# Cross-attention in a decoder layer: exponentials without maxima behind a check, keys by position a batch ahead, queries turned by VectorE and DRAM

## Chip, cores and metric

The kernel runs on one core of a Trainium2 chip. The metric is the device time of one execution in microseconds (us), lower is better. The engines are TensorE (PE; its weight loads are listed as PEld), VectorE (DVE), ScalarE (ACT), GpSimd (POOL) and the queue that issues most transfers, SyncE (SP).

## What is computed

One pre-norm decoder layer in fp32: x of 16 batches x 128 rows x 1024 columns, self-attention, cross-attention to a context of the same shape, and a feed-forward network (FFN) with int4 weights of inner width 2752. The change is in the cross-attention, which treats the 128 rows as channels (c) and the 1024 columns as positions (n):

```python
qh = jnp.einsum('bcn,oc->bon', q, Wq).reshape(b, HEADS, DIM_HEAD, -1)   # 8 heads of 64
kh = jnp.einsum('bcn,oc->bon', k, Wk).reshape(b, HEADS, DIM_HEAD, -1)
vh = jnp.einsum('bcn,oc->bon', v, Wv).reshape(b, HEADS, DIM_HEAD, -1)
qh = jax.nn.softmax(qh, axis=-2) * SCALE      # over the 64 features of a head
kh = jax.nn.softmax(kh, axis=-1)              # over the 1024 positions
context = jnp.einsum('bhdn,bhen->bhde', kh, vh)
out = jnp.einsum('bhde,bhdn->bhen', context, qh)
out = jnp.einsum('bcn,oc->bon', out.reshape(b, HIDDEN, -1), Wo) + bo[None, :, None]
norm = jnp.maximum(jnp.sqrt(jnp.sum(out * out, axis=1, keepdims=True)), 1e-12)
return out / norm * g * np.sqrt(DIM)
```

q is the layer-normalised x, k and v are the context. The result is added to x.

## The kernel before

The program has three stages on one core: self-attention in four groups of four batches (lines 289 to 510), cross-attention batch by batch (512 to 916), and the FFN, whose matrix products are done by a fast (Strassen-Winograd) scheme in blocks (918 to 1770). The stages overlap at their ends.

**Order of work.** `InOrder` (line 50) keeps TensorE's and VectorE's instructions in the order in which the program writes them. In cross-attention that order is made by a small clock: `later(n, fn)` puts a function on a list, `tick()` runs those that are due. A batch has four key units and four query units in turn, a tick after each: eight ticks. After the last batch each matrix product of the FFN's first block ticks once (`beside`), and when the list is empty `attention_done` closes the stage's pools and starts the preparation of the later FFN weights. SP issues its transfers in order; a transfer that waits holds up those behind it. Batches 8 to 15 come first, then 0 to 7.

**Key unit** (`key_unit`, line 669). It makes 128 of the 512 key features for all 1024 positions: two matmuls into a pair of PSUM banks (`kq`), the row maximum on VectorE (`knmax`), and the exponential with that bias and an accumulated sum on ScalarE (`ke`, line 678). The context product needs positions on the partitions, so two ticks later VectorE turns 32x32 blocks (`kt`), SP stores the tile in DRAM (`kd`, line 692) and loads it back with the blocks in place (`kh`, line 696).

**Query unit** (`query_unit`, line 701). It makes all 512 features for 256 positions, positions on the partitions: two matmuls, the maximum of each head (`qmx`), the subtraction on VectorE (`qe`), the exponential on ScalarE (line 715). Two ticks later `weigh` sums each head (`qden`), takes the reciprocal and lets GpSimd multiply (line 721). Four ticks later `turn` makes eight 128x128 transposes on TensorE (`tr`, with the identity), and two ScalarE copies (`qs`, line 731).

**The rest of a batch.** `context` multiplies the turned keys with the context (`mm<-kh,cxt`, 32 instructions of 256 columns for each batch; each fp32 matmul is recorded as two) and `mix` folds in the product of Wv and Wo (`g_sb`, made once) and the key sums' reciprocal, giving `m_sb`. `project_out` multiplies `m_sb` with the turned queries in four pieces, takes the column norms with a matmul against ones, and then scales, adds to x, takes the statistics for the FFN's normalisation and turns the rows for it (`turn_rows`, tile `xt`, through DRAM). Blocks of these rows are loaded for the FFN by `block_loads`.

Tile pools of the stage lie on two sides: those of the units (cx, weights, ke, kt, qe, and `kq` in four PSUM banks) are given back when the last unit is written, the others when `attention_done` runs.

Of the kernel before, what the change touches and what calls it, by code (L numbers as in the profile page):

```python
# [33 lines left out]
Q = 32  # L34

# [30 lines left out]
def decoder_layer(  # L66
# [22 lines left out]
    out: bass.AP,  # L89
):  # L90
    nc = tc.nc
# [474 lines left out]
    def turn_rows(b, xn, pool):  # L566

        kt = pool.tile([P, 4, 2 * JC, Q], F32, name="xt")
        vector.transpose(
            kt.rearrange("p c m t -> p m c t"), xn.rearrange("p m (c i) -> p m c i", c=4)  # L570
        )
        xt = xt_all[PASSES.index(b - b % HB)][b % HB]
        for a in range(4):
            nc.sync.dma_start(
                xt[a].rearrange("c i n j t -> i c (n j t)"),
                kt[ts(a, Q)].rearrange("i c m t -> i c (m t)"),
            )
# [21 lines left out]
    bkt = unit_pool("b_kt", 2)  # L599
    b3 = unit_pool("b_3", 3)  # L600
    bpk = unit_pool("b_k", 2, space=PSUM)
    bs = side_pool("b_s", 1)
    bct = side_pool("b_ct", 3)
    bkh = side_pool("b_kh", 3)
    bqs = side_pool("b_qs", 7)
    b1 = side_pool("b_1", 1)
    b2 = side_pool("b_2", 2)
    bps = side_pool("b_ps", 2, space=PSUM)
    btr = side_pool("b_tr", 2, space=PSUM)
# [16 lines left out]
    if True:  # L626
# [15 lines left out]
        vector.memset(ones, 1.0)  # L642

# [25 lines left out]
        def key_unit(c_sb, oc, kh, part, ksum):  # L669
            ps = bpk.tile([P, 2, 512], F32, name="kq")  # L670
            for h in range(2):
                tensor.matmul(
                    ps[:, h, :], wk_sb[:, ts(oc, P)], c_sb[:, ts(h, 512)], start=True, stop=True
                )
            nmax = small.tile([P, 1], F32, name="knmax")
            vector.tensor_reduce(nmax, ps, AX.XY, ALU.max, negate=True)
            ke = b0.tile([P, 2, 512], F32, name="ke")
            nc.scalar.activation(ke, ps, AF.Exp, bias=nmax, accum_out=ksum[:, oc : oc + 1])  # L678

            if oc % 2 == 0:
                part[:] = [dram.tile([4, Q, 4, 2, NB, Q], F32, name="kd", tag="kd", bufs=2)]
            (kd,) = part

            def turn():
                kt = bkt.tile([P, 4, NB, Q], F32, name="kt")
                vector.transpose(
                    kt.rearrange("p c n j -> p n c j"),
                    ke.rearrange("p h (n c j) -> p (h n) c j", c=4, j=Q),  # L690
                )
                nc.sync.dma_start(kd[:, :, :, oc % 2].rearrange("p i c n j -> (p i) c n j"), kt)
                if oc % 2 == 1:
                    t = kh[oc // 2] = bkh.tile([P, 4, 2, NB, Q], F32, name="kh")
                    for c in range(4):
                        nc.sync.dma_start(
                            t[ts(c, Q)], kd[:, :, c].rearrange("p i o n j -> i p o n j")
                        )

            later(2, turn)  # L700

        def query_unit(xn, pair, qs):
# [8 lines left out]
            mx = small.tile([P, 2 * HEADS], F32, name="qmx")  # L711
            vector.tensor_reduce(mx, heads, AX.X, ALU.max)
            qe = b3.tile(wide, F32, name="qe")
            vector.tensor_tensor(qe, heads, mx.unsqueeze(2).to_broadcast(wide), ALU.subtract)
            nc.scalar.activation(qe, qe, AF.Exp)

            def weigh():
                den = small.tile([P, 2 * HEADS], F32, name="qden")
                vector.tensor_reduce(den, qe, AX.X, ALU.add)
                vector.reciprocal(den, den)  # L720
                nc.gpsimd.tensor_tensor(qe, qe, den.unsqueeze(2).to_broadcast(wide), ALU.mult)  # L721

            def turn():
                qt = bqs.tile([P, 4, 2 * P], F32, name="qs", tag="qs")
                qs.append(qt)
                qf = qe.rearrange("p (i r e) d -> p i r (e d)", i=2, e=2)
                for i in range(2):
                    tr = btr.tile([P, 4, P], F32, name="tr")
                    for r in range(4):
                        tensor.transpose(tr[:, r, :], qf[:, i, r], ident)  # L730
                    nc.scalar.copy(qt[:, :, ts(i, P)], tr)

            later(2, weigh)
            later(4, turn)

        def context(ct, kh, ksum, m_sb, when):

            kc = b1.tile([P, HIDDEN], F32, name="kc")
            bank = {}

            def piece(pair, part):
                if part == 0:
                    bank[pair] = bps.tile([P, HIDDEN // 2], F32, name="mm")
                ps = bank[pair]
                for nb in range(4 * part, 4 * part + 4):
                    tensor.matmul(
                        ps,
                        ct[:, nb, :],
                        kh[pair][:, :, :, nb, :].rearrange("n p o j -> n (p o) j"),
                        start=(nb == 0),  # L750
                        stop=(nb == NB - 1),
                    )
                if part == 1:

                    nc.scalar.copy(
                        kc[:, ts(pair, HIDDEN // 2)].rearrange("s (o p j) -> s o p j", o=2, j=Q),
                        ps.rearrange("s (p o j) -> s o p j", o=2, j=Q),
                    )

            def mix():  # L760
                D = DIM_HEAD
                krec = small.tile([P, 4], F32, name="krec")
                vector.reciprocal(krec, ksum)
                mp = bps.tile([P, 4, S], F32, name="mm")
                for r in range(4):

                    for e in range(2):
                        tensor.matmul(
                            mp[ts(e, D), r, :],
                            kc[:, ds(r * P + e * D, D)],  # L770
                            g_sb[:, 2 * r + e, :],
                            start=True,
                            stop=True,
                        )
                vector.tensor_tensor(
                    m_sb, mp, krec.unsqueeze(2).to_broadcast([P, 4, S]), ALU.mult
                )

            for k in range(4):
                later(when[k], lambda k=k: piece(*divmod(k, 2)))  # L780
            later(when[4], mix)

        def turned(b):
# [8 lines left out]
            later(2, lambda: turn_rows(b, xn, b1))  # L792
# [6 lines left out]
        def project_out(b, qs, m_sb, when):  # L799
            out, bank = {}, {}  # L800

            def piece(h, part):
# [6 lines left out]
                for r in range(4):  # L809
                    tensor.matmul(  # L810
                        ps[:, ts(part, 2 * P)],
                        m_sb[:, r, :],
                        qs[2 * h + part][:, r, :],
# [70 lines left out]
        for n in range(2 * BPT):  # L884
# [3 lines left out]
            )  # L888
        for k, b in enumerate(batches):
            kh, part, qs = {}, [], []  # L890
            ksum = b2.tile([P, 4], F32, name="ksum")
            m_sb = b1.tile([P, 4, S], F32, name="m_sb")

            if k + 2 < B:
# [945 lines left out]
```

## Time and profile before

| | |
|---|---|
| median of three runs | 2272.14 us (2271.86 to 2274.11) |
| the profiled execution | 2272.22 us, its span 2270.4 us |
| TensorE clock granted | 1.00 throughout |
| self-attention | about the first 250 us |
| cross-attention | its first key matmul starts at 252.9 us, its last key matmul at 784.9, its last projection matmuls at about 842 |
| FFN | its first product starts at 794.4 us; from 847 to the end it has TensorE alone |
| vector work for one batch in cross-attention | knmax, qmx 1192 ns each, qe 1225, qden 1205, kt 1230, four times each |

The profile is one execution taken by the hardware profiler. Rows of groups give line, engine, operation, output and input tiles, shape and number of instructions, then busy time and the mean of one in ns. Line 62 is the `InOrder` helper, so most TensorE and VectorE instructions of the stage are told apart by their tiles. The end of a matmul is modelled[...], so that the pace of a sequence is read from the starts. A wait is given as who waited for whom, the sum in us, how often, and the longest.

### The profile page before, as it was taken

What the parts mean: (1) busy time and instruction counts of PE and PEld (TensorE: products, weight loads), DVE (VectorE), ACT (ScalarE), POOL (GpSimd) and SP (SyncE); (2) the same over time, 40 slices, a digit from 0 to 9 for tenths busy, and PEclk for the clock granted to TensorE, in tenths of its full rate; (3) what the DMA queues carried; (4) which work ended last, traced back from release to release, by engine and by line L of the source; (5) the groups of instructions that cost most, each with busy time, mean ns of one, the idle gap of its engine ahead of it and who ended that gap; (6) DMA issues with size and microseconds to landing.
All of it is one profiled execution on the core that took longest, in us unless ns stands there. A gap on an engine that the chain in (4) does not pass through costs nothing.

```text
span 2270.4 us, 25324 instructions
## 1 busy us (share of the span) xinstructions
PE 2243.3 (99%) x8968; PEld 1598.7 (70%) x8968; DVE 1616.5 (71%) x2161; ACT 546.2 (24%) x861; POOL 473.7 (21%) x381
## 2 busy tenths in 40 slices
PE   8999999999999999999999999999999999999999
PEld 7556566666666664444684468888888688888888
DVE  6987788889889938665796658777777546544463
ACT  2111255665665551111111111121121100000000
POOL 5452122222222200000340034444443000000000
PEclk9999999999999999999999999999999999999999
DMA  6445266566688558788739943554554974434631
GB/s 248 159 135 183 93 168 183 169 195 193 169 241 224 156 167 276 265 273 269 231 119 276 287 135 122 185 194 145 184 191 149 339 235 149 140 121 145 224 116 38
DMA packets 276974, 425.22 MB, mean 187 GB/s; under 512 B 26736, under 2 KB 128496, under 8 KB 276720
## 3 DMA queue, kind: packets, MB, share of 16 engines
q1 hardware_dynamic: 250768, 377.71, 53.2%
q0 software_dynamic: 8064, 27.27, 3.3%
q10 hardware_dynamic: 18016, 18.62, 2.6%
q8 instruction: 72, 1.18, 0.2%
q14 instruction: 54, 0.44, 0.1%
HBM read 265.62 MB, written 157.35 MB: 186 GB/s over the span
## 4 chain that ended last, share of the span: by engine, by line
PE 91%; DVE 6%; issue 2%; DMA 1%; ACT 1%; POOL 0%; SPq 0%; DVEq 0%; POOLq 0%; ACTq 0%
PE po L1725 21%; PE q L62 20%; PE p L62 18%; PE mm L62 11%; PE kq L62 8%; PE mm L391 4%; PE tr L62 2%; PE p L1102 2%; PE mm L406 2%; DVE pa L62 1%; PE mm L287 1%; PE tr L338 1%; DVE ti L62 0%; DVE bnst L62 0%; DVE kt L62 0%
## 5 line engine op out<-in xcount | busy, mean ns | idle before, releaser
L62 PE MATMUL p<-b,w 128*128 128x512 f32 x560 | 246.4, 592 | 0.0
L62 PE MATMUL q<-ti,li 128*128 128x256 f32 x1008 | 232.2, 379 | 3.5 <-DVE ti L62 2.8
L62 PEld LDWEIGHTS q<-ti,li 128*128 128x128 f32 x1008 | 191.0, 190 | 31.3 <-issue 2.8
L62 POOL TENSOR_TENSOR li<-w 128x512 f32<-128x512 f32 x84 | 118.2, 1409 | 430.8 <-DMA wu<-pc 235.6
L62 PEld LDWEIGHTS p<-b,w 128*128 128x128 f32 x560 | 106.4, 190 | 133.1 <-issue 128.7
L1725 PE MATMUL po<-wc,lc 128*128 128x256 f32 x840 | 183.4, 379 | 0.0
L721 POOL TENSOR_TENSOR qe<-qe,qden 128x1024 f32<-128x1024 f32 x64 | 121.7, 1901 | 270.0 <-DVE qden L62 160.7
L62 PE MATMUL p<-T,w 128*128 128x512 f32 x400 | 177.2, 592 | 0.0
L1725 PEld LDWEIGHTS po<-wc,lc 128*128 128x128 f32 x840 | 159.6, 190 | 21.8
L62 ACT COPY k<-q 128x512 f32<-128x512 f32 x126 | 73.8, 585 | 400.0 <-PE q L62 400.0
L62 PEld LDWEIGHTS p<-T,w 128*128 128x128 f32 x400 | 76.0, 190 | 95.7 <-issue 95.4
L1725 PE MATMUL po<-wq,lq 128*128 128x256 f32 x560 | 126.7, 379 | 0.3 <-issue 0.3
L62 PEld LDWEIGHTS mm<-qs,m_sb 128*128 128x128 f32 x512 | 97.2, 190 | 38.9 <-issue 28.2
L62 PE MATMUL kq<-cx,wk_sb 128*128 128x512 f32 x256 | 120.8, 594 | 3.7 <-ACT ke L678 3.7
L62 PE MATMUL mm<-kh,cxt 128*128 128x256 f32 x512 | 122.6, 382 | 1.0 <-PE mm L62 0.5
L62 PE MATMUL kq<-wq_sb,xn 128*128 128x512 f32 x256 | 120.4, 593 | 0.0
L62 PE MATMUL mm<-qs,m_sb 128*128 128x256 f32 x512 | 120.3, 379 | 0.0
L62 PEld LDWEIGHTS mm<-kh,cxt 128*128 128x128 f32 x512 | 95.9, 190 | 31.3 <-issue 18.6
L1725 PEld LDWEIGHTS po<-wq,lq 128*128 128x128 f32 x560 | 106.0, 190 | 15.9 <-issue 0.9
L62 DVE TENSOR_TENSOR pa<-pa,sz 128x1024 f32<-128x1024 int32 x86 | 112.6, 1309 | 2.5
L391 PE MATMUL mm<-xnT,wqkv_sb 128*128 128x512 f32 (+1 forms) x320 | 112.6, 508 | 0.0
L62 DVE TENSOR_REDUCE qmx<-kq 128x16 f32<-128x1024 f32 x64 | 76.3, 1192 | 47.6 <-PE kq L62 47.6
(191 smaller groups left out, 3858.7 us busy)
## 6 DMA issues: line engine op xcount, KB each, us to landing
w<-wu SPq DMA_DIRECT2D x140, 256.0 KB, 3.3
lq<-h SPq DMA_DIRECT2D x140, 256.0 KB, 4.5
w<-wg SPq DMA_DIRECT2D x138, 256.0 KB, 2.8
kd<-kt SPq DMA_DIRECT2D x64, 512.0 KB, 3.5
kh<-kd SPq DMA_DIRECT2D x128, 256.0 KB, 5.6
h<-hc SPq DMA_DIRECT2D x80, 256.0 KB, 2.9
wq<-wd SPq DMA_DIRECT2D x70, 256.0 KB, 5.0
h<-h SPq DMA_DIRECT2D x60, 256.0 KB, 3.4
```

The lines of the kernel that those rows point to most:

```text
L62: return lambda *args, **kw: self._tc.keep_in_program_order(fn(*args, **kw))
L287: tensor.matmul(ps, oT[:, d, ts(b % BPT, S)], wo_d[d][:, ts(h, 512)], start=(d == 0), stop=(d == 1),)
L338: nc.tensor.transpose(tr[:, j, :], xn[:, ts(4 * h + j, P)], ident)
L391: nc.tensor.matmul(ps[:, tokens], wqkv_sb[:, f, c, :], xnT[:, c, tokens], start=(c == 0), stop=(c == CC - 1),)
L406: nc.tensor.matmul(ps, xnT[:, c, ts(i, S)], wqkv_sb[:, 4:6, c, :], start=(c == 0), stop=(c == CC - 1),)
L721: nc.gpsimd.tensor_tensor(qe, qe, den.unsqueeze(2).to_broadcast(wide), ALU.mult)
L1102: tensor.matmul(ps, wt[:, j, :], T[q][:, :, j], start=(first == q and j == 0), stop=(q in (2, 3, 4) and j == JC - 1), skip_group_check=True,)
L1725: nc.tensor.matmul(bank[:, i, :], l[:, ts(i, S)], w,  start=(start and c == 0 and i % 2 == 0), stop=(stop and c == len(pairs) - 1), skip_g ...
```

## The change

Four things are changed in cross-attention.

- **No maxima.** With `plain` set, keys and queries are exponentiated as they come. The sums and their reciprocals are added up on GpSimd (`note`), and after the stage `raise_flag` counts the partitions in which both totals are at most 1e18. At the end of the program every engine reads that count; if it is below 128, the whole layer is run again with the maxima (`plain` unset), otherwise that second copy of the program is jumped over.
- **Keys by position.** A key unit now makes all 512 features for 256 positions, with positions on the partitions. The exponentials are used as they lie, as the moving operand of the context product with 512 columns (`use`); key sums over positions are added on VectorE and finished on TensorE by matmuls against a column of ones in `mix`. The keys' trip through DRAM goes.
- **A batch ahead.** Key units for the next batch stand between the query units of this one; four key units with four ticks stand before the first batch. In the last batch there are query units alone.
- **Queries through VectorE and DRAM.** `turn` now transposes 32x32 blocks on VectorE (`kt`), stores to DRAM (`kd`), and a tick later loads four pieces (`qs`). The transposes on TensorE and the ScalarE copies go. The projection reads `qs` in runs of 32 elements.

The times in ticks of the later steps, the pools and their numbers of buffers follow. The diff, cut to its core:

```diff
-    bkt = unit_pool("b_kt", 2)
+    bek = unit_pool("b_ek", 3)
+    bas = unit_pool("b_as", 1)
     b3 = unit_pool("b_3", 3)
+    bkt = side_pool("b_kt", 3)
...
-    bct = side_pool("b_ct", 3)
-    bkh = side_pool("b_kh", 3)
-    bqs = side_pool("b_qs", 7)
+    bct = side_pool("b_ct", 2)
+    bqs = side_pool("b_qs", 5)
...
-    bps = side_pool("b_ps", 2, space=PSUM)
-    btr = side_pool("b_tr", 2, space=PSUM)
+    bps = side_pool("b_ps", 3, space=PSUM)
...
+        def note(*both):
+            if plain:
+                for t, v in zip(totals, both):
+                    t = t[:, : v.shape[1]]
+                    nc.gpsimd.tensor_tensor(t, t, v, ALU.add)
+
+        def raise_flag():
+
+            within = [small.tile([P, 1], F32, name=f"within{n}") for n in range(2)]
+            for w, t in zip(within, totals):
+                vector.tensor_reduce(w, t, AX.X, ALU.add)
+                vector.tensor_scalar(w, w, LIMIT, None, ALU.is_le)
+            vector.tensor_tensor(within[0], within[0], within[1], ALU.mult)
+            ps = bps.tile([P, 1], F32, name="mm")
+            tensor.matmul(ps, ones, within[0], start=True, stop=True)
+            vector.tensor_copy(flag, ps[0:1])
...
+        def key_unit(ctx, p, st):
...
             ps = bpk.tile([P, 2, 512], F32, name="kq")
-            for h in range(2):
+            for i in range(2):
+                chunk = c_sb[:, ts(2 * p + i, P)]
+                if plain:
+                    tensor.matmul(ps[:, i, :], chunk, wk_sb, start=True, stop=True)
+                    continue
...
+            ek = bek.tile([P, 2, 512], F32, name="ek")
+            nc.scalar.activation(ek, ps, AF.Exp)
+
+            def use():
+                if p == 0:
+                    st["ps"] = bps.tile([P, HIDDEN], F32, name="kx", bufs=1)
+                    st["ek"] = ek
+                for i in range(2):
+                    tensor.matmul(
+                        st["ps"],
+                        ct[:, 2 * p + i, :],
+                        ek[:, i],
+                        start=(p == i == 0),
+                        stop=(p == 3 and i == 1),
+                    )
+                if p == 1:
+                    st["sum"] = bas.tile([P, 2, 512], F32, name="ksum")
+                    vector.tensor_tensor(st["sum"], st["ek"], ek, ALU.add)
+                elif p > 1:
+                    vector.tensor_tensor(st["sum"], st["sum"], ek, ALU.add)
+                if p == 3:
+                    t = st["sum"]
+                    vector.tensor_tensor(t[:, 0], t[:, 0], t[:, 1], ALU.add)
+                    st["kc"] = b1.tile([P, HIDDEN], F32, name="kc")
+                    nc.scalar.copy(st["kc"], st["ps"])
+                    later(2, lambda: mix(st))
+
+            later(2, use)
+
+        def mix(st):
+
+            D = DIM_HEAD
+            ks = bps.tile([P, 4], F32, name="mm")
+            for r in range(4):
                 tensor.matmul(
+                    ks[:, r : r + 1], st["sum"][:, 0, ts(r, P)], ones[:, 0:1], start=True, stop=True
                 )
+            ksum, krec = (small.tile([P, 4], F32, name=name) for name in ("ksum", "krec"))
+            vector.tensor_copy(ksum, ks)
+            vector.reciprocal(krec, ksum)
+            note(ksum, krec)
...
             qe = b3.tile(wide, F32, name="qe")
-            vector.tensor_tensor(qe, heads, mx.unsqueeze(2).to_broadcast(wide), ALU.subtract)
-            nc.scalar.activation(qe, qe, AF.Exp)
+            if plain:
+                nc.scalar.activation(qe, heads, AF.Exp)
...
             def turn():
-                qt = bqs.tile([P, 4, 2 * P], F32, name="qs", tag="qs")
-                qs.append(qt)
-                qf = qe.rearrange("p (i r e) d -> p i r (e d)", i=2, e=2)
-                for i in range(2):
-                    tr = btr.tile([P, 4, P], F32, name="tr")
-                    for r in range(4):
-                        tensor.transpose(tr[:, r, :], qf[:, i, r], ident)
-                    nc.scalar.copy(qt[:, :, ts(i, P)], tr)
+                kt = bkt.tile([P, 4, NB, Q], F32, name="kt")
+                vector.transpose(
+                    kt.rearrange("p c n j -> p n c j"),
+                    qe.rearrange("p h d -> p (h d)").rearrange("p (n c j) -> p n c j", c=4, j=Q),
+                )
+                kd = dram.tile([4, Q, 4, NB, Q], F32, name="kd", tag="kd", bufs=3)
+                nc.sync.dma_start(kd.rearrange("a i c n j -> (a i) c n j"), kt)
+
+                def load():
+                    qt = qs[pair] = bqs.tile([P, 4, NB, Q], F32, name="qs", tag="qs")
+                    for c in range(4):
+                        nc.sync.dma_start(
+                            qt[ts(c, Q)], kd[:, :, c].rearrange("a i n j -> i a n j")
+                        )
+
+                later(1, load)
 
             later(2, weigh)
-            later(4, turn)
+            later(wait, turn)
...
-                        m_sb[:, r, :],
-                        qs[2 * h + part][:, r, :],
+                        st["m"][:, r, :],
+                        qs[2 * h + part].rearrange("p a (i r) j -> p r i a j", r=4)[:, r],
...
+            if len(ahead) == 2:
+                when = (12, 13, 14, 15, 16, 1, 1)
+            elif ahead:
+                when = (12, 13, 14, 15, 16, 1, 0)
             else:
-                when = (8, 9, 11, 12, 13), (14, 14, 15, 15, 16, 1, 0)
+                when = (10, 10, 11, 11, 12, 1, 0)
...
             for oc in range(4):
+                if ahead:
+                    key_unit(ctxs[ahead[0]], oc, keys[ahead[0]])
+                    tick()
+                query_unit(xns[b], oc, qs, 4 if len(ahead) == 2 else 3)
                 tick()
...
-        decoder_layer(tc, *args, res)
+        with tc.tile_pool(name="flag", bufs=1) as fp:
+            flag = fp.tile([1, 1], I32, name="flag")
+            decoder_layer(tc, *args, res, flag)
+            rows_within = nc.values_load(flag, min_val=0, max_val=P)
+
+            with tc.If(rows_within < P):
+                decoder_layer(tc, *args, res)
```

## Prediction

> **What bounds the kernel now.** I read the page's busy shares first, then the busy time by stretches, then one cross-attention batch in order of time on TensorE, then the waits of TensorE and of the SP queue.
>
> ```profile
> PE 2243.3 (99%) x8968; PEld 1598.7 (70%) x8968; DVE 1616.5 (71%) x2161; ACT 546.2 (24%) x861; POOL 473.7 (21%) x381
> ...
> PE 91%; DVE 6%; issue 2%; DMA 1%; ACT 1%; POOL 0%; SPq 0%; DVEq 0%; POOLq 0%; ACTq 0%
> ```
>
> TensorE is busy for all but 27 us. A busy PE need not be at its peak, so the next two views check it where the change is made. Stretches (columns: stretch, length, then busy us of PE, PEld, DVE, ACT, POOL with instruction counts, clock, DMA share, GB/s):
>
> ```profile
> 290.00:310.00 20.00, 16.93 (x64) 9.48 (x62) 18.93 (x22) 10.79 (x18) 6.26 (x4) 1.00 0.54 152
> ...
> 435.66:469.65 33.99, 33.99 (x150) 23.09 (x149) 29.99 (x36) 20.48 (x33) 8.79 (x6) 1.00 0.64 186
> 469.65:503.64 33.99, 33.99 (x149) 23.08 (x149) 29.99 (x36) 20.49 (x33) 8.78 (x6) 1.00 0.65 187
> ```
>
> A batch takes 33.99 us, with no hole on PE and VectorE (DVE) at 30.0. Only the first batches have holes. Inside a batch (start, length, what):
>
> ```profile
> 503.48 1.89 PE L62 MATMUL mm<-qs,m_sb 128*128 128x256 f32 x8
> 505.20 1.89 PE L62 MATMUL mm<-kh,cxt 128*128 128x256 f32 x8
> 506.93 1.04 PE L62 MATMUL tr<-ident,qe 128*128 128x128 f32 x8
> 507.80 1.88 PE L62 MATMUL kq<-wq_sb,xn 128*128 128x512 f32 x4
> 509.52 1.89 PE L62 MATMUL mm<-kh,cxt 128*128 128x256 f32 x8
> 511.25 1.88 PE L62 MATMUL kq<-cx,wk_sb 128*128 128x512 f32 x4
> 512.96 1.88 PE L62 MATMUL mm<-sq,ones 128*128 128x512 f32 x4
> ```
>
> Start to start, every group takes its columns at one rate: 4 passes of 512 in 1.72 us, 8 passes of 256 in 1.73, 8 transposes of 128 in 0.87 (506.93 to 507.80). An fp32 matmul is two passes, a transpose one. So this stage costs what TensorE is given, and a change is worth the passes that it removes. What PE waits for, and what SP waits for (sum us, times, longest us):
>
> ```profile
> PE kq L62 <- ACT ke L678: 3.7, 4, 1.6
> PE q L62 <- DVE ti L62: 3.3, 4, 2.4
> PE p L1102 <- DMA w<-wg: 1.7, 1, 1.7
> ```
> ```profile
> SPq L692 <- DVE kt L62: 280.8, 51, 16.0
> ...
> SPq L696 <- DMA kd<-kt: 69.0, 32, 3.2
> ```
>
> PE loses 3.7 us to key exponentials, all but 0.2 in the first batch, and 1.7 to the FFN's first weights. SP waits a lot, but in the stage's batches PE waits for what it then moves (kh) only once, for 0.2 us.
>
> **What the Trainium skill says.** "TensorE: Matmul & The Clock Gate", LDWEIGHTS, prices a weight load by its columns over 1.2, which is 107 ns for 128; the trace agrees in that 16 passes of 128 columns with a load each (line 421) took 1.78 us, 111 ns each. "VectorE: DVE Perf Modes", The three transpose paths, says that VectorE turns 32x32 blocks only, so a full turn needs another mover: here the kt groups (1230 ns for 128x1024) plus a store and loads through DRAM. "DMA: Bandwidth & Descriptors", Two DMAs through the same engine are not ordered, has the issuing engine wait for the first DMA's completion: the 69.0 us above. "Runtime: NRT & Kernel Launch", Instruction fetch mechanics, says that a taken branch to far code stalls for a fetch; no branch is in this trace.
>
> **The change, part by part** (16 batches).
>
> 1. *Query turns leave TensorE.* 4 units x 8 transposes per batch, 0.87 us per unit: 0.872 x 64 = 55.8 us removed, nothing of it beside other PE work. -55.8. The 128 ACT copies of them (593 ns) go too; ACT is not on the path.
>
> 2. *Key sums on TensorE.* The maxima's accumulated sums go; mix has four matmuls of one column, eight passes per batch. Each needs a 128-column load; with one column to compute, the load sets the pace. The trace shows no such matmul. Page price 107 ns: 128 x 0.107 = 13.7 us, which I take. Low end: the issue floor of the same page (Back-to-back issue gap, about 25 ns), 3.2 us. High end: the duration that the trace shows of one load, 190 ns, 24.3 us. **+13.7 (3 to 24)**. These wait for DVE's last half add of the sum; behind them on PE stand that mix and the next unit. DVE has from tick 8 to tick 2, two units and more on PE, for some 6 us of queued work, so I cost the wait at nothing; uncovered it would be at most the 1.2 + 0.7 us of those adds per batch.
>
> 3. *Context product.* 32 passes of 256 per batch become 16 of 512; by the rows above 1.73 against 1.72 us for the same columns. 0. The projection reads qs in runs of 32 floats as the context product read kh before, at the same 1.73. 0.
>
> 4. *DVE, ACT, POOL.* DVE loses per batch four knmax (1192 ns), four qmx (1192) and four qe subtractions (1225), 14.4 us, and gains three adds (1.22) and a half one (0.69), 4.4; the four transposes move from keys to queries. 30.0 - 14.4 + 4.4 = 20.0 us of a new period of 33.99 - 3.49 + 0.86 = 31.4. POOL gets ten small adds per batch: between 0.10 us (a one-element memset) and 1.03 (pow on four columns), so 1 to 10 us on top of 8.8; under 31.4 even so. All this is hidden by PE. If a tick's POOL work slips, the turn behind it slips, which is the rival below.
>
> 5. *DRAM trip.* SP issues per batch 4 kd stores, 16 qs loads, 4 xt, 2 ctx = 26 instead of 18; at about 0.45 us an issue (four take 1.73 to 1.75 us in SP's timeline) 12 us of 31. The loads wait for their store, with the next stores and ctx loads queued behind, but they now come a tick after it rather than at once. From the last turn (tick 11) to its use (tick 15) PE has nine 1.72 us groups, 15.5 us. The trip needs a transpose 1.23, store landing 3.5 and load landing 5.6 (the median of the larger kh loads): 10.3. Spare 5 us: 0.
>
> 6. *Start.* With keys a batch ahead and no maxima, an exponential follows its matmul at once and its bank comes free earlier. The four waits above and their like in the first 80 us (PE busy 73.8 of 80) should mostly go; the prologue of four key units may bring its own. **-3.5 (-5 to 0)**. The FFN's first weight tile waits for space that the last keys' input held; these keys now end a batch earlier. **-1 (-1.7 to 0)**.
>
> 7. *The flag.* raise_flag puts five small DVE ops and a matmul in program order in the FFN's first block: PE stands, with all later products behind it, until DVE has done them. Ahead on DVE is the last xt transpose (1.23) and up to two 0.69 us combinations. 1.23 + about 1.2 (five ops near the 253 ns of a 16-element reciprocal) + a PE drain of 0.17 = 2.6, plus half of a combination. **+3 (1 to 5)**.
>
> 8. *Branch at the end.* Every engine reads the flag and jumps over a second copy of the program. Not in the trace; the last matmul group starts at 2265.47 and the last outputs are issued at 2266.9, so part of it lies beside the 3.5 us of the last outputs' transfer. I take **+4 (1 to 10)**: one round trip of about a DMA landing (3 us) plus synchronisation. A gain is excluded, since the old end stays.
>
> Sum: -55.8 + 13.7 - 3.5 - 1 + 3 + 4 = -39.6. The profiled execution took 2272.2 us (span 2270.4, 1.8 around it), the same as the median of 2272.1: **2232.6 us**.
>
> **Rivals.**
> - *The trip sets the end (slower side).* Place: pieces at ticks 12 to 15, where PE meets qs. It costs only beyond 15.5 us; then each batch waits once. With 20 us: 15 batches x 4.5 = 68, so 2232.6 + 68 = 2300. It decides against the change from 15.5 + 39.6/15 = 18.1 us. For: SP's queue is in order and longer, DMA share reaches 0.81 and 0.90 in the stretches around 622 to 690. Against: same bytes as before, DVE is relieved, 5 us spare.
> - *Part of the gain is lost in small waits* (DVE, POOL or qs, 1 us per batch): 2232.6 + 16 = 2249. For: DVE order holds scale, weigh, turn and mix together at ticks 1 and 2. Against: 11 us of DVE slack per batch.
> - *More than forecast:* one-column matmuls near the floor (-10.5), flag and branch at their low ends (-5): 2217.
> - *The check fails and the general path runs:* about twice the time, 4500. Exponentials of normalised rows times weights of unit gain are far below 1e18, so hardly.
>
> **How the numbers follow.** Forecast 0.72 (its own range 2222 to 2245), small waits 0.13, more gain 0.10, trip 0.04, general path 0.01. Low end: between the forecast's low and the third rival; high end takes in the second: 2220 to 2252. About 0.2% is what a measurement here can tell from no change. Faster 0.95, same 0.01, slower 0.04.
>
> **What would show it.** Right: no tr<-ident,qe group; a period near 31.4 us with PE full; mix longer by 0.86 us; DVE near 20 us per period. Wrong: PE waiting for DMA qs (trip), for DVE sum (step 2), or a tail of more than 10 us after the last output (step 8). A second set of self-attention groups means the general path.

## The result, and the profile after

The kernel after the change takes 2265.88 us (2260.47 to 2271.04) against 2273.52 us before on the same chips: ratio 0.9965, interval 0.9955 to 0.9974. It is faster, by 0.35%; the forecast was 2232.6 us, 1.7%, and the time lies outside the range. The profiled execution took 2262.39 us with a span of 2260.5, against 2272.22 and 2270.4 before: 9.8 us gained where 39.6 were forecast. The question is where 29.8 us went. The profiled execution is one of the shorter ones of fourteen: their mean granted clock lies between 0.992 (the longest, 2271.04 us) and 0.997 (the shortest, 2260.47), and the median moved by 7.6 us only.

The busy shares and the chain of the page after:

```profile
PE 2207.0 (98%) x8330; PEld 1517.4 (67%) x8330; DVE 1517.2 (67%) x2055; ACT 472.0 (21%) x651; POOL 555.6 (25%) x543
...
PE 86%; DVE 6%; DMA 3%; issue 3%; SPq 1%; ACT 1%; POOL 1%; DVEq 0%; POOLq 0%; ACTq 0%
```

TensorE has 638 fewer instructions (512 transposes and 256 of the context product gone, 128 for the key sums and two for the flag added) and 36.3 us less busy time, but it stands still for 53.5 us of the span where that was 27. So the work left TensorE as the sum said, and much of it came back as waiting. DMA is now 3% of the chain, and SP's queue is on it. What TensorE waits for, in order of size (sum us, times, longest; left out is a wait at the program's start):

```profile
PE mm L63 <- DMA qs<-kd: 21.2, 10, 4.3
...
PE p L1156 <- DMA w<-wg: 5.7, 2, 5.5
PE q L63 <- DVE ti L63: 3.3, 4, 2.4
PE mm L63 <- DVE within L63: 2.4, 1, 2.4
```

The first line is new: TensorE reaches the projection and the turned queries have not come back from DRAM, ten times. The second is the FFN's first weight tile, 1.7 us before; the third was there before; the last is the flag. Now one batch in order of time on TensorE (start, length, what, wait before it):

```profile
504.34 1.88 PE L63 MATMUL kq<-wq_sb,xn 128*128 128x512 f32 x4
506.06 0.95 PE L63 MATMUL mm<-ones,ksum 128*128 128x1 f32 x8
506.94 1.09 PE L63 MATMUL mm<-g_sb,kc 128*64 128x128 f32 x16
...
525.26 1.88 PE L63 MATMUL kq<-wk_sb,cx 128*128 128x512 f32 x4
529.04 1.97 PE L63 MATMUL mm<-qs,m_sb 128*128 128x256 f32 x8 [1.90 <-DMA qs<-kd]
```

The key sums take 506.06 to 506.94, 0.88 us for eight passes. The same wait came at 395.61 and at 595.92, six batches apart: 200.31 / 6 = 33.4 us for a batch, against 33.99 before and 31.4 forecast. Three stretches: one of those shown before the change, one around the wait at 595.92, and one without a wait (columns: stretch, length, busy us of PE, PEld, DVE, ACT, POOL, clock, DMA share, GB/s):

```profile
435.66:469.65 33.99, 31.89 (x111) 17.89 (x110) 24.66 (x29) 16.55 (x21) 14.04 (x17) 1.00 0.65 191
574.00:606.00 32.00, 29.89 (x94) 16.43 (x91) 21.81 (x26) 14.12 (x17) 11.88 (x16) 0.95 0.58 173
608.00:639.23 31.23, 31.23 (x109) 17.78 (x108) 24.35 (x29) 16.17 (x19) 13.60 (x16) 1.00 0.87 245
```

From 608.00 to 639.23 lies a whole batch without a wait: 31.2 us with TensorE full, the forecast period. In the stretch from 574 to 606 the granted clock falls to 0.95; in the first, which also holds a wait (2.10 us, at 462.19), it stays at 1.00. What differs between the two kinds of batch is seen on SP's queue (start, time in which the entry had the queue, what, number). A batch with a wait:

```profile
509.95 13.20 SPq L817 DMA_DIRECT2D kd<-kt  x3
523.24 4.08 SPq L822 DMA_DIRECT2D qs<-kd  x8
```

and one without:

```profile
619.10 0.33 SPq L817 DMA_DIRECT2D kd<-kt  x1
619.52 2.20 SPq L822 DMA_DIRECT2D qs<-kd  x4
622.25 2.31 SPq L822 DMA_DIRECT2D qs<-kd  x4
624.77 0.34 SPq L817 DMA_DIRECT2D kd<-kt  x1
```

In the first, three stores are queued one after another, and the loads of two pairs behind the third. The three stores wait for these turns on VectorE:

```profile
508.69 1.23 DVE L63 STREAM_TRANSPOSE kt<-qe 128x1024 f32<-128x1024 f32 x1
...
515.88 1.25 DVE L63 STREAM_TRANSPOSE kt<-qe 128x1024 f32<-128x1024 f32 x1
...
521.57 1.23 DVE L63 STREAM_TRANSPOSE kt<-qe 128x1024 f32<-128x1024 f32 x1
```

A pair is the 256 positions of one query unit. Counted in ticks, the first of these turns is that of a batch's last pair, the other two are those of the first two pairs of the next batch. In all ten waits it is the fourth and last piece of a batch's projection that waits, and each time SP has such a row of three stores ahead of the loads.

The first store could go at 509.95 and lands in 3.0 us (the page's median for kd), at about 513; its loads are issued at 523.24, behind a store that only the turn at 521.57 releases. They stand about 10 us in the queue for data that have nothing to do with them. The program writes each load a tick after its store; the scheduler that places transfers on SP need not keep that order, since only TensorE and VectorE have an `InOrder`.

**Theory A**, before the experiments: this order on SP is the cause of the 21.2 us, and the slow clock follows from the waits. **Rivals**: the trip itself takes too long for the place it has; the clock falls by itself, with the new mix of work; the check's small additions on GpSimd, which stand ahead of each multiplication of the queries, delay the turn. The expectations below name them by letters and repeat what each says.

### The profile page after: what moved, and what is told of

It is laid out like the page before. It is cut to its first block, busy times and chain, and to the rows that moved or that the text cites. A ratio compares the mean times of both kernels' runs of the same rounds, so it can differ in the third digit from the quotient of the medians.

```text
span 2260.5 us, 24112 instructions
## 1 busy us (share of the span) xinstructions
PE 2207.0 (98%) x8330; PEld 1517.4 (67%) x8330; DVE 1517.2 (67%) x2055; ACT 472.0 (21%) x651; POOL 555.6 (25%) x543
## 3 DMA queue, kind: packets, MB, share of 16 engines
q1 hardware_dynamic: 244624, 377.72, 53.5%
## 4 chain that ended last, share of the span: by engine, by line
PE 86%; DVE 6%; DMA 3%; issue 3%; SPq 1%; ACT 1%; POOL 1%; DVEq 0%; POOLq 0%; ACTq 0%
PE po L1779 21%; PE q L63 20%; PE p L63 18%; PE kq L63 8%; PE mm L63 6%; PE kx L63 4%; PE mm L396 4%; DMA qs<-kd 2%; PE mm L411 2%; PE p L1156 1%; DVE pa L63 1%; PE mm L292 1%; SPq L822 1%; DVE kt L63 1%; PE tr L343 1%
## 5 line engine op out<-in xcount | busy, mean ns | idle before, releaser
L1779 PEld LDWEIGHTS po<-wc,lc 128*128 128x128 f32 x840 | 159.6, 190 | 21.7
L63 PE MATMUL mm<-qs,m_sb 128*128 128x256 f32 x512 | 123.0, 384 | 21.2 <-DMA qs<-kd 21.2
L805 POOL TENSOR_TENSOR qe<-qe,qrec 128x1024 f32<-128x1024 f32 x64 | 132.1, 2064 | 4.0 <-issue 0.2
L63 PE MATMUL kx<-ek,cxt 128*128 128x512 f32 x256 | 121.8, 598 | 0.0
L63 PE MATMUL kq<-wk_sb,cx 128*128 128x512 f32 x256 | 120.4, 592 | 0.0
L726 ACT ACTIVATE ek<-kq 128x1024 f32<-128x1024 f32 x64 | 65.5, 1023 | 182.1 <-PE kq L63 182.1
L63 DVE TENSOR_REDUCE qden<-qe 128x16 f32<-128x1024 f32 x64 | 76.4, 1194 | 29.6 <-ACT qe L794 29.6
```

The source lines that it names most:

```text
L63: return lambda *args, **kw: self._tc.keep_in_program_order(fn(*args, **kw))
L726: nc.scalar.activation(ek, ps, AF.Exp)
L805: nc.gpsimd.tensor_tensor(qe, qe, rec.unsqueeze(2).to_broadcast(wide), ALU.mult)
L1779: nc.tensor.matmul(bank[:, i, :], l[:, ts(i, S)], w,  start=(start and c == 0 and i % 2 == 0), stop=(stop and c == len(pairs) - 1), skip_g ...
```

## Experiments

Ratios are to the kernel before, with 95% intervals.

**1. The stores and loads in the written order** (`e1_order`). SP gets the helper that TensorE has:

```diff
     tensor, vector = InOrder(tc, nc.tensor), InOrder(tc, nc.vector)
+    sync = InOrder(tc, nc.sync)
...
-                nc.sync.dma_start(kd.rearrange("a i c n j -> (a i) c n j"), kt)
+                sync.dma_start(kd.rearrange("a i c n j -> (a i) c n j"), kt)
...
-                        nc.sync.dma_start(
+                        sync.dma_start(
                             qt[ts(c, Q)], kd[:, :, c].rearrange("a i n j -> i a n j")
```

> The changed kernel with one edit: kd stores and qs loads keep on SP the order in which the program writes them (each pair's loads ahead of the next pair's store). Theory A (the loads of the last pair stand in SP's queue behind the next batch's first store, which waits for a later DVE turn): TensorE's waits for qs fall from 21.2 us to under 3, the mean clock rises from 0.992-0.997 to 0.998 or more because no idle gap is left to lower it, 2232 to 2245 us. Theory B (the trip itself, with DVE and POOL work ahead of it, is longer than the 15.5 us that it has): waits stay above 15 us, 2258 to 2268. Theory C (the clock falls by itself, whatever the waits): waits go, the clock stays near 0.994, 2244 to 2250.

Measured: 2249.73 us, 0.9895 (0.988 to 0.991). SP's queue in a batch, where each load now follows one store:

```profile
498.01 0.34 SPq L63 DMA_DIRECT2D kd<-kt  x1
501.89 1.73 SPq L63 DMA_DIRECT2D qs<-kd  x4
505.22 0.34 SPq L63 DMA_DIRECT2D kd<-kt  x1
...
512.85 3.68 SPq L63 DMA_DIRECT2D qs<-kd  x4
516.57 0.43 SPq L63 DMA_DIRECT2D kd<-kt  x1
```

No wait of TensorE for qs is left, and its largest waits in cross-attention and after are:

```profile
PE mm L63 <- DVE within L63: 10.1, 1, 10.1
...
PE p L1157 <- DMA w<-wg: 8.9, 1, 8.9
```

The stretches after this edit:

```profile
574.00:606.00 32.00, 32.00 (x112) 18.21 (x111) 25.11 (x30) 16.14 (x19) 13.60 (x16) 1.00 0.77 230
...
734.00:766.00 32.00, 23.14 (x80) 12.57 (x79) 22.86 (x32) 12.10 (x15) 15.64 (x22) 0.89 0.68 207
```

With the order alone changed, the same number of bytes and the same ticks, the 21.2 us are gone and a batch takes 31.2 us, so theory A holds for the waits, and that the trip in itself is too long falls. For the clock the numbers alone do not decide: theory C also expected the waits to go, a clock near 0.994 (it is 0.995 here) and 2244 to 2250 us. The stretches decide against it. From 337.97 us on, thirteen batches follow one another in 31.23 us each, the clock is 1.00 in the stretch where it was 0.95, and it is low only where two long waits now stand, at the seam to the FFN.

The time missed the 2232 to 2245 us of theory A because those two waits grew. TensorE comes to the FFN's first weight tile 28.6 us earlier than before this edit and to the flag 21.7 us earlier, but these are ready only 25.2 and 14.0 us earlier: waits of 8.9 and 10.1 us where they were 5.5 and 2.4. That is 11.1 us given back, before the slow clock behind them is counted.

**2. The pieces of the projection a tick later** (`e2_late`). This gives the trip more time and leaves SP's queue to the scheduler:

```diff
             if len(ahead) == 2:
-                when = (12, 13, 14, 15, 16, 1, 1)
+                when = (13, 14, 15, 16, 17, 1, 1)
```

> The changed kernel with the four output pieces and the norms one tick (about 3.9 us) later in all batches but the last two; SP's order is left as it was. Theories A and B both: the waits for qs of 1.9 to 4.3 us go in these batches, 2235 to 2247 us; this prices the waits with what they do to the clock, and does not tell A from B. Theory C: waits go, clock stays near 0.994, 2244 to 2250.

Measured: 2268.49 us, 0.9977 (0.9966 to 0.9987), and the wait is not smaller:

```profile
PE mm L63 <- DMA qs<-kd: 26.9, 12, 4.2
```

This expectation was wrong. One batch on SP, VectorE and TensorE says why:

```profile
511.56 13.95 SPq L817 DMA_DIRECT2D kd<-kt  x3
525.61 4.11 SPq L822 DMA_DIRECT2D qs<-kd  x8
```
```profile
523.92 1.25 DVE L63 STREAM_TRANSPOSE kt<-qe 128x1024 f32<-128x1024 f32 x1 [1.96 <-POOL qe L805]
```
```profile
531.52 1.97 PE L63 MATMUL mm<-qs,m_sb 128*128 128x256 f32 x8 [2.19 <-DMA qs<-kd]
```

The expectation took a tick for 3.9 us. But when all four pieces move by a tick, only one more group of 1.7 us stands ahead of the fourth: from the query unit of the tick in which the first piece was due before (511.50 us in the changed kernel, 511.98 here) TensorE now comes to it after 17.35 us instead of 15.64. And the loads still stand behind the third store, whose turn waits for GpSimd here, so that they are issued 13.63 us after that unit instead of 11.74. The later use won 1.7 us and the loads came 1.9 us later; why the turn is later was not tested.

**3. Queries turned on TensorE, the rest of the change kept** (`e3_pe_turn`, `e8_pe_turn_mm`). Eight transposes and two ScalarE copies again for each unit, as before the change; in the first with one PSUM bank of its own (`mm` gives one up), in the second in the three banks of `mm`.

```diff
             def turn():
+                qt = qs[pair] = bqs.tile([P, 4, 2 * P], F32, name="qs", tag="qs")
+                qf = qe.rearrange("p (i r e) d -> p i r (e d)", i=2, e=2)
+                for i in range(2):
+                    tr = bps.tile([P, 4, P], F32, name="tr", tag="mm")
+                    for r in range(4):
+                        tensor.transpose(tr[:, r, :], qf[:, i, r], ident)
+                    nc.scalar.copy(qt[:, :, ts(i, P)], tr)
```

> The changed kernel with the queries turned by TensorE transposes again (one PSUM bank for them, two ScalarE copies a unit), no kd or qs trip; keys, missing maxima and check stay. All theories: TensorE has 55.8 us more work and no wait for qs; from 2235 without waits to 2285-2295 us, slower than before, since the key part alone adds 13.7 us of one-column matmuls and 5 to 6 us of check. If it comes out near 2265 the key part saves time that I do not see.

> As e3_pe_turn, with the transposes' results in the three shared PSUM banks instead of one of their own. If the 77 us that TensorE waited there for ScalarE's copies came from the single bank, they fall below 10, and the time is that of the sum, 2285 to 2300 us: keys and missing maxima by themselves cost time while TensorE sets the pace, and the whole gain of the change is in the 55.8 us of transposes. Otherwise above 2340.

Measured: 2379.34 us, 1.0464 (1.0448 to 1.048), with one bank; 2287.51 us, 1.0062 (1.0046 to 1.0077), with the shared ones. The first is far off because of the bank, not of the transposes:

```profile
PE tr L63 <- ACT qs L818: 77.2, 62, 2.3
```

The second four transposes of each unit wait until ScalarE has copied the first four, 1.25 us each time. In the second kernel this wait is gone (3.6 us for transposes in all). It tells what the rest of the change is worth alone: 0.6% slower than before. By the forecast's own terms the rest is +13.7 - 3.5 - 1 + 3 + 4 = +16.2; measured is 0.0062 x 2273 = +14. So all of the gain comes from the 55.8 us of transposes that leave TensorE (`e8_pe_turn_mm` takes 53.0 us more than `e6_order_w_flag` below, on the same chip), and the order of the queues decides how much of it is kept.

**4. Without the check** (`e4_no_check`). No sums of the sums, no flag, no branch, no second copy of the program:

```diff
-    plain = flag is not None
+    plain = True
...
-            if plain:
-                for t, v in zip(totals, both):
-                    t = t[:, : v.shape[1]]
-                    nc.gpsimd.tensor_tensor(t, t, v, ALU.add)
+            return
...
-            if plain:
-                raise_flag()
```

> The changed kernel without totals, flag, branch and second copy of the layer (the general path is left out). Theories A, B and C: 2.4 us of TensorE's wait for the flag and 2.7 us at the end go, about 2260 to 2262 us, and the waits for qs stay near 20 us. Rival D (the small GpSimd adds hold up DVE and GpSimd and so make the trip late): the waits for qs fall below 8 us and the time to 2240-2250.

Measured: 2254.33 us, 0.9917 (0.9904 to 0.9931), some 11 us less than with the check and below the 2260 to 2262 us that theories A, B and C gave. The wait that this was to test stays:

```profile
PE mm L63 <- DMA qs<-kd: 18.9, 10, 3.9
```

So GpSimd's additions are not what makes the queries late; the wait is smaller by 0.23 us each time, which is about one such addition (0.22 us at 518.37 in the changed kernel). Of the 11 us, 2.6 lie at the end (from the start of the last matmul group to the end of the span 5.0 us, with the check 7.7), 2.4 are the flag's wait, 2.3 are in the line above; the other 4 are spread. The mean clock of the profiled execution is 0.998 here and 0.996 with the check, which over 2250 us comes to some 4 us (an estimate from these figures); no run tells whether the check is the reason for that. Where the seam is in better order (the next experiment's kernel with and without the check) the check costs 5.6 us.

**5. The seam to the FFN.** Three kernels follow up the waits that the first experiment uncovered. `e5_order_w` adds to the first experiment that SP, in written order, loads the FFN's first four weight tiles. The first of them was on GpSimd's queue, behind the last queries' multiplications; the others were on SP before, in the scheduler's order:

```diff
-            load_weights(nc.gpsimd if n == 0 else nc.sync)
+            load_weights(sync)
```

> e1_order with the FFN's first weight tile loaded by SP, not by GpSimd, where it stands behind the last queries' multiplications. Theory A (queues set it): TensorE's wait of 8.9 us for that tile falls to under 3 and the clock dip after it goes, so 2238 to 2244 us; the 10.1 us for the flag stay. Rival (the weights were waiting for the space of the last unit's tiles, not for the queue): wait stays near 9, 2247 to 2251.

Measured: 2235.52 us, 0.9833 (0.982 to 0.9847): 14 us less. The wait for the tile is gone, 8.9 us, with the slow group behind it (5.30 us for 3.60 in `e1_order`), 1.7 us, and the flag's wait is 1.7 us shorter, 8.4; the other 2 us are not told apart. `e6_order_w_flag` then moves the flag's matmul into the FFN's second block, where VectorE has long finished (`inside` keeps the result until then, `one` is a column of ones):

```diff
-            ps = bps.tile([P, 1], F32, name="mm")
-            tensor.matmul(ps, ones, within[0], start=True, stop=True)
-            vector.tensor_copy(flag, ps[0:1])
+            return within[0]
...
+            if blk == 1 and n == 3 and inside:
+                ps = banks[0].tile([P, TB], F32, name="pf", tag="gu")[0:1, 0:1]
+                tensor.matmul(ps, inside.pop(), one, start=True, stop=True)
+                vector.tensor_copy(flag, ps)
```

> As e5_order_w, and the flag's matmul is moved from the end of the stage into the FFN's second block, where VectorE's five small operations are long done. Theory A: the 10.1 us wait for the flag and the slow clock after it go as well, 2226 to 2233 us, a mean clock of 0.999 or more: the sum of the forecast without waits. If VectorE's other work would have stopped TensorE there anyway: 2236 to 2242.

Measured: 2234.51 us, 0.9831 (0.9817 to 0.9844): 1 us less, which the runs cannot tell from nothing. The last sentence of its expectation came true: VectorE's other work stops TensorE there anyway. The wait did not go, it changed its name. TensorE, and VectorE ahead of it:

```profile
820.57 6.00 PE L1158 MATMUL p<-b,w 128*128 128x512 f32 x8 [8.97 <-DVE h L63]
```
```profile
811.20 1.22 DVE L63 SCALAR_TENSOR_TENSOR y<-sq,y 128x1024 f32<-128x1024 f32 x1 [24.83 <-ACT sq L879]
812.46 1.28 DVE L63 SCALAR_TENSOR_TENSOR X<-y,gs_sb,X 128x1024 f32<-128x1024 f32 x1
...
816.26 0.68 DVE L63 TENSOR_TENSOR h<-p,k 128x512 f32<-128x512 f32 x1
```

VectorE, in written order, stands 24.8 us with the last batch's norms at the head of its queue, which ScalarE can make only when TensorE has done the last projection piece (at 803.70) and the matmul for its squares (at 807.14). The FFN's combinations `h` are queued behind it, and TensorE's next products need their banks. The flag's operations come after them in the same queue (819.14 here), so its waits of 10.1 and 8.4 us were most likely this one. `e7_order_w_no_check` is `e5_order_w` without the check.

> As e5_order_w without totals, flag, branch and second copy of the layer (the general path is left out). Price of the check where nothing else waits: against e6_order_w_flag only the end, 2.7 us, and some GpSimd time: 2223 to 2231 us. If the check costs more than that (11.6 us were seen between the changed kernel and e4_no_check), below 2220.

Measured: 2229.95 us, 0.9812 (0.9799 to 0.9826), with 8.2 us of wait for `h` where there is no flag: the stall at the seam is not the check's.

**6. The last batch's norms later on VectorE** (`e9_steps3`, `e10_steps5`). To `e6_order_w_flag`:

```diff
-                when = (10, 10, 11, 11, 12, 1, 0)
+                when = (10, 10, 11, 11, 12, 3, 0)
```

and 5 in place of 3 in the second. The number is the delay, in ticks, from the last batch's norms to what follows them: VectorE scales the output by the norm, adds it to x and takes the statistics. The first expectation calls these steps the queries' scaling, additions and turn; the edit does not touch those.

> As e6_order_w_flag (the key stores and query loads in the written order on SyncE, the FFN's first weight tiles on SyncE, the flag's one-column matmul in the FFN), and the last batch alone does its queries' scaling, note additions and turn 2 ticks later, so that the FFN's first VectorE operations stand ahead of the 24.8 us wait for ScalarE. Theory A (what is left beside the DRAM trip is one place on VectorE's queue at the seam to the FFN): the 9.0 us wait of TensorE for h goes, and with it the slow pace after it (about 2 us): 2222 to 2229 us, ratio 0.978 to 0.981. Rival B (the wait only moves: the preparation of the last queries starts later, and another wait of the same size takes its place): 2232 to 2240, 0.983 or above.

> As e9_steps3 with the last batch's step 4 ticks later instead of 2. Theory A: 2222 to 2229 us like e9_steps3, if 2 ticks were too few there, lower than e9_steps3 by the wait that is left. Rival B: 2232 to 2245, and later than e9_steps3, as the last results come later to the FFN.

Measured: 2239.82 us, 0.9847 (0.9833 to 0.986), and 2238.25 us, 0.9839 (0.9826 to 0.9853), against 0.9831 without it: not faster. Rival B's range was met, and a wait did move, though not because the last queries' preparation started later. The wait for `h` is 5.4 us in the first and gone in the second, where the groups after the seam run without a gap:

```profile
813.10 3.60 PE L1158 MATMUL p<-b,w 128*128 128x512 f32 x8
816.53 7.03 PE L63 MATMUL p<-b,w 128*128 128x512 f32 x16
...
1137.43 3.54 PE L63 MATMUL q<-ti,li 128*128 128x256 f32 x8 [2.44 <-DVE ti L63]
1295.60 3.78 PE L63 MATMUL q<-ti,li 128*128 128x256 f32 x8 [10.36 <-POOL li L63]
```

At the first `q` group this kernel is 9.9 us ahead of `e6_order_w_flag` (1058.91 against 1068.79 us). At 1295.60 TensorE waits 10.4 us, a wait that `e6_order_w_flag` does not have, for GpSimd's combinations of prepared weights, and GpSimd waits for VectorE:

```profile
1292.11 1.76 POOL L63 TENSOR_TENSOR li<-w 128x512 f32<-128x512 f32 x1 [13.17 <-DVE pa L63]
```

So the theory was right about the place: the seam's wait goes and TensorE runs ahead. But the preparation of a later weight takes it all back 480 us later. `e6_order_w_flag` comes to the same group at about 1293.4 us (it is the second half of its row of 16 from 1291.64), so this kernel, which was 9.9 us ahead, is now 2.2 us behind, and the groups after the wait are slow again.

The edit itself may have made the preparation late. It begins when the list of ticks is empty, and a longer delay in the last batch empties the list later: VectorE's first operation of it (`pa<-raw`) comes, counted from 800 us on, after two of the FFN's combinations `h<-p,k` in `e6_order_w_flag`, at 821.15 us, and after four such combinations here, at 823.81, although TensorE is some 10 us ahead. No run separates this from TensorE's lead.

Of all versions with the check `e6_order_w_flag` and `e5_order_w` are the fastest (0.9831 and 0.9833).

## Why the prediction was wrong

The step that failed is step 5: "they now come a tick after it rather than at once", "The trip needs a transpose 1.23, store landing 3.5 and load landing 5.6 (...): 10.3. Spare 5 us: 0." The landings were costed too long, if anything: kd lands in 3.0 us and qs in 4.1 (medians). What was not costed is the load's place in SP's queue. The step counted how many issues SP has and read the tick of the code as the order of the queue, though only TensorE's and VectorE's instructions are kept in written order. The sum for one trip in the trace is 1.23 + 3.0 + some 10 in the queue + about 2 for its four issues + 4.1 = 20.3 us, 508.69 to 529.04; TensorE's work filled 18.4 of them. The rival "the trip sets the end" named this place and this queue ("SP's queue is in order and longer"), but let it decide only when every batch waits 2.6 us or more; ten waits of 2.1 us took half of the gain and not all. The rival "small waits" had qs among them, but stopped at 1 us per batch and 2249 us. The prediction's own sign of being wrong, TensorE waiting for DMA qs, is what the trace shows.

The steps one by one, forecast and measured (us, profiled executions):

| step | forecast | measured |
|---|---|---|
| 1 transposes | -55.8 | no such group is left; 0.87 x 64 stands, and experiment 3 agrees |
| 2 key sums | +13.7 | +14.1 (506.06 to 506.94, times 16) |
| 3 context in 512 columns | 0 | 0 (1.72 us a group) |
| 4 VectorE, GpSimd | 0 | no wait of its own on TensorE; VectorE at 24.3 of 31.2, not 20.0 |
| 5 DRAM trip | 0 | +21.2 of waits, and at least +3.6 of slow groups behind two of them |
| 6 start | -3.5 | -4.7 (250 to 330 us: TensorE busy 78.4, 73.8 before) |
| 6 FFN's first weight | -1 | +4.0, and +1.5 for the slow group behind it |
| 7 flag | +3 | +2.4 |
| 8 branch | +4 | +2.7 (7.68 from the last group to the end, 4.93 before) |

The measured terms sum to -55.8 + 14.1 + 21.2 + 3.6 - 4.7 + 4.0 + 1.5 + 2.4 + 2.7 = -11.0; the profiled time moved by -9.8. Two losses stand outside the table: 1.5 in self-attention (TensorE is busy for 238.1 of the first 250 us, 239.6 before) and 1.5 in a slow group at 1174.34 us, 3.32 us long instead of 1.80. With them the sum is -8.0, and 1.8 us of the gain are not accounted for.

Step 2 took the price of a weight load, 107 ns, from the Trainium skill ("TensorE: Matmul & The Clock Gate", LDWEIGHTS); the trace now gives 0.88 / 8 = 0.11 us for each one-column pass, so that price was right and the issue floor was not reached. Step 4 missed 4.3 us on VectorE. VectorE operations with two inputs in SBUF stretch where GpSimd works:

```profile
502.83 2.25 DVE L63 SCALAR_TENSOR_TENSOR y<-sq,y 128x1024 f32<-128x1024 f32 x1 [0.87 <-ACT sq L877]
...
514.01 1.85 DVE L63 SCALAR_TENSOR_TENSOR shift<-mv,rstd 128x1 f32<-128x1 f32 x1
...
519.63 2.01 DVE L63 TENSOR_TENSOR ksum<-ksum,ek 128x1024 f32<-128x1024 f32 x1 [1.11 <-ACT ek L726]
```

GpSimd multiplies queries at 502.10 to 504.00, 513.08 to 515.85 and 518.66 to 520.56; elsewhere the same forms take 1.18 us (y, before the change), 0.14 (shift, before the change) and 1.23 (ksum, at 494.81). The Trainium skill, "SBUF — State Buffer", SBUF: two separate sides, says that a VectorE operation with two SBUF inputs and a GpSimd operation share one pair of ports, and that the later one blocks until the first is done; these rows agree with that, and no run here tests it by itself. The three stretches are 1.1, 1.7 and 0.8 us, 3.6 of the 4.3. Only the last is in one of the added operations; the other two were there before the change and meet GpSimd now. The last one reaches the DRAM trip: the turn at 521.57 that releases the third store follows this ksum directly on VectorE, so up to 0.8 of the 1.9 us of wait at 529.04 may come from it. With the order on SP kept no such wait is left.

Step 6 looked at the space for the first weight tile and not at its queue. The tile is issued by GpSimd, behind the last batch's query multiplications; `e5_order_w` shows it, since the same load on SP's queue has no wait. In `e1_order` GpSimd issues it at 753.69 us, directly after a multiplication that starts at 751.67, and TensorE has been waiting since 751.3.

The slow clock had no term at all. After the wait that ends at 595.92 two groups take 5.2 us instead of 3.44:

```profile
595.92 2.56 PE L63 MATMUL mm<-qs,m_sb 128*128 128x256 f32 x8 [2.10 <-DMA qs<-kd]
598.28 3.02 PE L63 MATMUL kq<-wq_sb,xn 128*128 128x512 f32 x4
601.14 1.88 PE L63 MATMUL mm<-sq,ones 128*128 128x512 f32 x4
```

After a wait of the same length at 462.19 the pace is the usual one, 1.81 us for the group:

```profile
462.19 1.97 PE L63 MATMUL mm<-qs,m_sb 128*128 128x256 f32 x8 [2.10 <-DMA qs<-kd]
464.00 1.88 PE L63 MATMUL kq<-wq_sb,xn 128*128 128x512 f32 x4
```

The slow group at 1174.34 stands behind a wait of 2.44 us that the kernel before has too (1188.53), and there it was followed by the usual pace. So a slow pace follows waits in these traces, but not every one, and what decides is not shown.

Right were the direction, the place of the gain, the period of an undisturbed batch (31.2 for 31.4), and with the order on SP kept and the first weights moved, the total: `e5_order_w` takes 2235.5 us. That agreement is partly chance: it holds 8.4 us of wait at the seam where the forecast had 3 for the flag, so the other terms together came out some 2.5 us lower than forecast.

What stays open: why the scheduler orders SP's queue well in some batches and badly in ten, what decides whether a wait is followed by a slow pace, 4 us of the check's cost in `e4_no_check`, and whether the preparation of later weights could be brought forward to use the 9.9 us that `e10_steps5` wins and loses.

## What to carry to other kernels

A load that moves from "at once" to "a tick later" is only later in the program; look in the trace at what stands ahead of it on its issuing queue, and price the longest wait of that, not the number of issues. When a stage is made faster, each first transfer and each in-order queue at its end must come forward with it: here 11.1 us of the first experiment's gain came back at one seam, and all of the last one's at a weight that other engines prepare. A removed wait is a gain only if what TensorE meets next is already there.

## What had not been expected of the hardware

- A wait of TensorE of some 2 us can be followed by a slow pace: after 2.10 us (595.92) the next two groups took 1.8 us more than usual; after the same 2.10 us at 462.19 the next took 1.81 instead of 1.73 us, hardly more. The sixty-two waits of `e3_pe_turn`, 1.25 us on average, left the clock at 0.997 over the span, but behind the one of 2.28 us (299.96) a group of 1.72 us took 3.25. The Trainium skill, "TensorE: Matmul & The Clock Gate", Why this matters for your kernels, advises to keep gaps under about 3 us; here shorter ones were enough at times, and the measurement decides.
- A single PSUM bank for the transposes, shared in turn by TensorE and ScalarE, cost 2379.34 - 2287.51 = 91.8 us over the same work in three shared banks; 77.2 of them are recorded as waits for the copies.
- A check with a branch over a whole second copy of the program is cheap at the end: 2.7 us from the last matmul group on, and 5.6 us in all between `e5_order_w` and `e7_order_w_no_check`.
